# A four-layer kernel on one core: the values' pointwise products move ahead of a sample's depthwise convolutions

## The chip, the cores and the metric

The kernel runs on one core of one Trainium2 chip. Time is device microseconds (us) of that core. Before the change three runs took 4082.22, 4084.47 and 4076.9 us; the median is 4082.22 us. The profile shows one further execution, of 4084.82 us.

## The reference

Four layers act on `x` of shape (2, 128, 64, 64), each as `x = x + layer(groupnorm(x))`. The change is in layer 0:

```python
xn = biasfree_ln(x, ln1_w)
qkv = conv1x1(xn, w_qkv)                       # 128 -> 640 channels, pointwise
qkv = conv_general_dilated(qkv, w_dw, ..., feature_group_count=5 * c)   # 3x3 depthwise
q1, k1, v, q2, k2 = jnp.split(qkv, 5, axis=1)
...
q1, q2, k1, k2 = map(l2norm_tokens, (q1, q2, k1, k2))
attn1 = softmax(einsum('bhnc,bhmc->bhnm', q1, k1) * temperature)     # tokens x tokens
out1 = einsum('bhnm,bhmc->bhnc', attn1, v)
attn2 = softmax(einsum('bhnc,bhnd->bhcd', q2, k2) * temperature)     # channels x channels
out2 = einsum('bhnc,bhcd->bhnd', v, attn2)
out = conv1x1(biasfree_ln(conv1x1(out1 + out2, w_po), ln2_w), w_proj) + b_proj
```

Layer 1 is a set of small convolutions and correlations, layer 2 a quaternion product in the Fourier domain, layer 3 an attention with eight heads. The change does not touch them.

## The kernel before

Layer 0 (`_layer0`, L1449) treats the two samples one after the other. For each it normalizes the input into `xn` (channels on partitions, 4096 tokens), then runs `convolutions` (L1697), then `attention` (L1831), a long loop of TensorE, ScalarE and VectorE. `finish` (L1939) makes the output of a sample from `q1`, `v` and `w2`. For sample 0 it is not run on its own: it is the generator `before`, and sample 1's `convolutions` draws six steps of it after its first depthwise product and the rest after its second.

Inside `convolutions` each of the five groups of 128 channels is treated in two halves of 32 rows. A half takes two operations.

- `pointwise` (L1580) multiplies `xn` with the group's weights on TensorE: a halo row of 64 columns, then 512, 1024 and 512 columns. ScalarE copies each result (L1598) out of PSUM into a frame, a half with a border of zeros, which GpSimd sets by three memsets (L1582 to L1585).
- The 3x3 depthwise step is done in one of two ways. Seven halves go through TensorE (`depthwise`, L1604): 144 products with diagonal 32x32 blocks, L1613. Three halves, the first half of `k1` and both halves of `v`, go through VectorE (`taps`, L1640): a multiplication, L1648, and eight multiply-adds, L1650, on the frame.

The list `order` gives the seven TensorE halves: (1,1), (0,0), (0,1), (3,0), (4,0), (3,1), (4,1), as (group, half); groups 0 to 4 are q1, k1, v, q2 and k2. In step n of the loop TensorE does depthwise n, then the pointwise product of step n+2. A depthwise result is emptied from PSUM by ScalarE and VectorE together. For q1 and k1 `in_place` (L1626) makes sixteen copies, eight on each (L1633). For q2 and k2 `copy` (L1622, issued as L1624) makes two, one on each, into the pair `qk2`. Then ScalarE sums squares (L1638). At the end of each step VectorE does some of the taps: in sample 0, 5, 5, 5, 4, 4 and 4 of them, in sample 1, 2, 6, 6, 4, 4 and 4. One tap of `k1` is done before the first depthwise. After step 2 VectorE computes the inverse norms nq and nk (L1502, with GpSimd's power L1404) and their product `sc` (L1760), and after step 3 it scales `q1` (L1764).

PSUM has eight banks here. Six form three pairs, handed out in turn by `sp()`. Every depthwise takes two pairs, the first of them emptied by ScalarE and the second by VectorE. A pointwise product takes one pair, besides the two single banks, `acc(0)` and `acc(1)`. The other users of the pairs in this stage are the transposes of values and of the pair, and `finish` through `half()`.

In SBUF the frames for TensorE have the tag `pad` (two buffers) and the frames for VectorE the tag `vpad` (two buffers). The keys' frame takes one `vpad` buffer, so the frame of the second values' half waits for the end of the keys' taps. `qk2` has one buffer of 4096 elements, first written in step 3.

In this stage the program's own order holds on TensorE, VectorE, ScalarE and GpSimd: `_in_order` (L1328) ties each instruction to the one before it on its engine. DMAs, on SyncE's queue, are not tied in this way. The copies of layer 2's weights, L794, begin after sample 0's convolutions, whose last instruction is VectorE's product `own` (L1769).

Of the kernel before, what the change touches and what calls it, by code (L numbers as in the profile page):

```python
# [10 lines left out]
F32 = mybir.dt.float32  # L11
# [5 lines left out]
B, C, H, W = 2, 128, 64, 64  # L17
S = H * W
CH = 512
# [1429 lines left out]
def _layer0(ctx, tc, X, a, cst, worst, there, dram):  # L1449
# [13 lines left out]
    def acc(n):  # L1463
        return banks[:, 6 + n, :]
# [31 lines left out]
    v = one.tile([128, S], F32, name="v")  # L1496
# [3 lines left out]
    def inverse_norm(ss, name):  # L1500
        n = small.tile([128, 1], F32, tag=name, name=name)
        nc.vector.tensor_reduce(n, ss, AX.X, ALU.add)  # L1502
        _power(nc, small, n, n, 1e-24, 0.0, mhalf)
        return n
# [72 lines left out]
    def frame(pool, tag="pad", bufs=2):  # L1577
        return pool.tile([128, H // 2 + 2, W + 2], F32, tag=tag, name=tag, bufs=bufs)

    def pointwise(pad, grp, half):  # L1580

        nc.gpsimd.memset(pad[:, :, 0:1], 0.0)  # L1582
        nc.gpsimd.memset(pad[:, :, W + 1 : W + 2], 0.0)
        edge = 0 if half == 0 else H // 2 + 1
        nc.gpsimd.memset(pad[:, edge, :], 0.0)  # L1585
        first, to = (0, 1) if half == 0 else (H // 2 - 1, 0)
        for r0, n in ((4 * ROWS, 1), (0, ROWS), (ROWS, 2 * ROWS), (3 * ROWS, ROWS)):
            ps = sp() if n > ROWS else acc(int(r0 == 0)).rearrange("p (o c) -> p o c", o=1)
            for i in range(0, n, ROWS):
                rows = min(ROWS, n - i)  # L1590
                nc.tensor.matmul(  # L1591
                    ps[:, i // ROWS, : rows * W],
                    w_qkv[:, grp * C : (grp + 1) * C],
                    xn[:, (first + r0 + i) * W : (first + r0 + i + rows) * W],
                    start=True,
                    stop=True,
                )
            nc.scalar.copy(  # L1598
                pad[:, to + r0 : to + r0 + n, 1 : W + 1],
                ps.rearrange("p k (h w) -> p (k h) w", w=W)[:, :n, :],  # L1600
            )
            yield

    def depthwise(grp, pad):  # L1604


        ps = [sp() for _ in range(2)]
        for t in range(9):
            for c in range(4):
                for r in range(4):  # L1610
                    rows, to = slice(32 * r, 32 * r + 32), slice(32 * c, 32 * c + 32)
                    y0 = c * ROWS + t // 3
                    nc.tensor.matmul(  # L1613
                        ps[r // 2][to, r % 2, :].rearrange("p (h w) -> p h w", w=W),
                        diag[rows, grp, t, :],
                        pad[rows, y0 : y0 + ROWS, t % 3 : t % 3 + W],
                        start=(t == 0),
                        stop=(t == 8),
                    )
        return ps  # L1620

    def copy(out, in_):  # L1622
        turn[0] += 1
        (nc.scalar.copy if turn[0] % 2 else nc.vector.tensor_copy)(out, in_)  # L1624

    def in_place(ps, half, out, p):  # L1626


        for i in range(4):
            for n, engine in enumerate((nc.scalar.copy, nc.vector.tensor_copy)):  # L1630
                r, c = 2 * n + p, (i + 2 * n) % 4
                cols = slice((4 * half + c) * CH, (4 * half + c + 1) * CH)
                engine(out[32 * r : 32 * r + 32, cols], ps[n][32 * c : 32 * c + 32, p, :])  # L1633

    def squares(pool, t, at):
        junk = pool.tile([128, 2 * CH], F32, tag="junk", name="junk", bufs=1)
        n = t.free_size()
        nc.scalar.activation(junk[:, :n], t, AF.Square, accum_out=at)  # L1638

    def taps(grp, half, to, pad):  # L1640

        cols = slice(half * S // 2, (half + 1) * S // 2)
        out = to[:, cols].rearrange("p (h w) -> p h w", w=W)
        for t in range(9):
            x = pad[:, t // 3 : t // 3 + H // 2, t % 3 : t % 3 + W]
            tap = wd[:, 9 * grp + t : 9 * grp + t + 1]
            if t == 0:
                nc.vector.tensor_scalar_mul(out, x, tap)  # L1648
            else:
                nc.vector.scalar_tensor_tensor(out, x, tap, out, ALU.mult, ALU.add)  # L1650
            yield

    def squares_of(pool, out, half, at):
        for i in range(2 * half, 2 * half + 2):
            squares(pool, out[:, i * 2 * CH : (i + 1) * 2 * CH], at[:, i : i + 1])
# [41 lines left out]
    def convolutions(pool, b, before):  # L1697


        ss = small.tile([128, 2, 4], F32, tag="ss", name="ss")  # L1700
        ss2 = small.tile([128, 2, 4, 2], F32, tag="ss2", name="ss2")
        gram = None
        order = [(1, 1), (0, 0), (0, 1), (3, 0), (4, 0), (3, 1), (4, 1)]
        kpad = frame(pool, "vpad")
        run(pointwise(kpad, 1, 0))
        first = taps(1, 0, k1, kpad)
        frames = [frame(pool) for _ in range(2)]
        run(pointwise(frames[0], *order[0]))
        next(first)
        run(pointwise(frames[1], *order[1]))  # L1710
        by_vector = first

        def values_of(half):
            pad = frame(pool, "vpad")
            run(pointwise(pad, 2, half))
            return taps(2, half, v, pad)

        qk = None
        for n, (grp, half) in enumerate(order):
            ps = depthwise(grp, frames.pop(0))  # L1720
            following = iter(())
            if n + 2 < len(order):
                frames.append(frame(pool))
                following = pointwise(frames[-1], *order[n + 2])
            if grp >= 3:
                if grp == 3:
                    qk = pool.tile([128, 2, 4, CH], F32, tag="qk2", name="qk2", bufs=1)
                for p in range(2):
                    copy(qk[:, grp - 3, 2 * p : 2 * p + 2, :], ps[p])
                run(following)  # L1730
                for r in range(4):
                    squares(pool, qk[:, grp - 3, r, :], ss2[:, grp - 3, r, half : half + 1])
            else:
                out = (q1, k1)[grp]
                in_place(ps, half, out, 0)
                next(following, None)
                in_place(ps, half, out, 1)
                run(following)
                squares_of(pool, out, half, ss[:, grp, :])
            if n == 0:  # L1740
                by_vector = chain(by_vector, values_of(0))
                for _ in range(FIRST_PART):
                    next(before, None)
            elif n == 1:
                run(before)
            if n == 4:
                gram = acc(1)
                run(products(pool, qk, 0, gram))
            elif n == 5:
                run(value_tiles(0))  # L1750
            elif n == 6:
                run(value_tiles(1))
                run(products(pool, qk, 1, gram))
            if n == 2:
                squares_of(pool, k1, 0, ss[:, 1, :])
                by_vector = chain(by_vector, values_of(1))
                nq = inverse_norm(ss[:, 0, :], "nq1")
                nk = inverse_norm(ss[:, 1, :], "nk1")
                sc = small.tile([128, 1], F32, tag="sc", name="sc")
                nc.vector.scalar_tensor_tensor(sc, nq, nk, temp, ALU.mult, ALU.mult)  # L1760
            if n == 3:
                for c in range(0, NCH, 2):
                    cols = slice(c * CH, (c + 2) * CH)
                    nc.vector.tensor_scalar_mul(q1[:, cols], q1[:, cols], sc)  # L1764
            for _ in range(((5, 5, 5, 4, 4, 4, 0), (2, 6, 6, 4, 4, 4, 0))[b > 0][n]):
                next(by_vector, None)

        own = small.tile([128, 4, C], F32, tag="own", name="own", bufs=1)
        nc.vector.tensor_mul(  # L1769
            own,  # L1770
            gram.rearrange("p (r c) -> p r c", r=4),
            blocks.unsqueeze(1).to_broadcast([128, 4, C]),
        )
        return ss2, own
# [207 lines left out]
    def run(gen):  # L1982
        for _ in gen:
            pass

    def chain(*gens):
        for g in gens:
            yield from g
# [3 lines left out]
    with _in_order(tc):  # L1992
        first = normalize(0)
# [585 lines left out]
```

## Time and profile before

| What | us |
|---|---|
| median of three runs | 4082.22 |
| profiled execution, whole | 4084.82 |
| its span, first to last instruction | 4082.9 |
| start, normalization of sample 0 (0 to 33) | 33.0 |
| convolutions of sample 0 (33 to 190) | 157.0 |
| attention of sample 0 (190 to 790) | 600.0 |
| convolutions of sample 1 with the finish of sample 0 (790 to 985) | 195.0 |
| attention of sample 1 and finish (985 to 1614) | 629.0 |
| layers 1 and 2 (1614 to 2212) | 598.0 |
| layer 3 (2212 to 4083) | 1871.0 |

TensorE is busy for 95% of the span, VectorE for 78% and ScalarE for 79%. The stages are cut by hand at the rows where one kind of work gives way to another. A timeline row shows when a run of equal instructions starts, how long it is busy, engine and source line, what it writes and reads, how many there are, and in brackets how long the engine was idle before it and whose work ended that. A float32 matmul counts as two instructions, and a few matmul records can be missing.

### The profile page before, as it was taken

How to read it: one execution, taken by the hardware profiler on the slowest of the kernel's cores; microseconds unless marked ns; L12 is line 12 of the kernel's file. 1: busy time of each engine (PE TensorE's matmuls, PEld its weight loads, DVE VectorE, ACT ScalarE, POOL GpSimd, SP SyncE). 2: the span in 40 equal slices, each digit the busy share in tenths (PEclk: the TensorE clock that was granted, in tenths of full speed). 3: DMA queues.
4: the chain of work that ended last, by engine and by line, in shares of the span. 5: the costliest groups of instructions: out<-in, count | busy, mean ns of one | idle time of the engine just before them, and what ended most of it. 6: DMA issues, size and time to landing. Idle time of an engine off the chain costs nothing.

```text
span 4082.9 us, 82128 instructions
## 1 busy us (share of the span) xinstructions
PE 3876.2 (95%) x35214; PEld 1325.1 (32%) x35214; DVE 3195.3 (78%) x3572; ACT 3245.5 (79%) x3955; POOL 71.1 (2%) x145
## 2 busy tenths in 40 slices
PE   7899999989999998997898999999999999999998
PEld 4511221244111113445665232232223223222222
DVE  5699898766899998986776887777777777776666
ACT  4488888735888984334654899999999999999998
POOL 1000000010000001000000000000000000000000
PEclk9999999999999999998899999999999999999999
DMA  1199970000000000003673210121012000110000
GB/s 50 23 193 187 189 95 2 1 2 2 1 2 2 2 2 13 6 1 128 256 278 112 72 35 29 36 61 32 24 32 70 27 27 29 36 54 6 6 6 4
DMA packets 193128, 217.59 MB, mean 53 GB/s; under 512 B 30441, under 2 KB 154345, under 8 KB 188658
## 3 DMA queue, kind: packets, MB, share of 16 engines
q1 hardware_dynamic: 192754, 212.25, 20.4%
q8 instruction: 278, 4.55, 0.5%
q14 instruction: 96, 0.79, 0.1%
HBM read 178.64 MB, written 98.57 MB: 68 GB/s over the span
## 4 chain that ended last, share of the span: by engine, by line
PE 63%; DVE 8%; issue 3%; ACT 1%; SPq 0%; DMA 0%; POOL 0%; DVEq 0%; POOLq 0%; ACTq 0%
PE ps_acc L2294 25%; PE ps_s L2271 18%; PE ps L1842 5%; PE ps L1850 5%; DVE X L662 3%; PE ps_bank L710 2%; PE ps_z L1008 2%; DVE e L950 1%; DVE sums L1873 1%; PE ps_bank L1062 1%; PE ps_bank L681 1%; PE ps_acc L2152 1%; PE ps_acc L2198 1%; PE ps_pe L925 1%; ACT weights L1923 1%
## 5 line engine op out<-in xcount | busy, mean ns | idle before, releaser
L2285 ACT ACTIVATE weights<-ps_s 128x1024 f32<-128x1024 f32 x1920 | 1781.5, 1062 | 76.0 <-PE ps_s L2271 75.9
L2294 PE MATMUL ps_acc<-weights,vt 128*32 128x512 f32 x8192 | 1092.9, 605 | 0.0
L1873 DVE TENSOR_TENSOR sums<-sums,weights 128x2048 f32<-128x2048 f32 x384 | 852.1, 2284 | 0.1
L2271 PE MATMUL ps_s<-q,k 64*128 64x512 f32 x4096 | 830.3, 469 | 4.2 <-DMA k<-stack 3.0
L1923 ACT ACTIVATE weights<-ps 128x1536 f32<-128x1536 f32 x512 | 741.0, 1447 | 8.5 <-PE ps L1850 8.5
L2271 PEld LDWEIGHTS ps_s<-q,k 64*128 64x128 f32 x4096 | 348.3, 184 | 936.4 <-ACT weights L2285 809.0
L1850 PE MATMUL ps<-q,k 32*64 32x512 f32 x8192 | 574.9, 613 | 3.8 <-ACT weights L1918 3.2
L1842 PE MATMUL ps<-weights,vt 128*32 128x512 f32 x4096 | 549.0, 608 | 0.0
L2243 DVE SCALAR_TENSOR_TENSOR exp_z<-exp_z,exp_m 128x1024 f32<-128x1024 f32 x384 | 469.0, 1221 | 9.3
L1918 ACT ACTIVATE weights<-ps 128x512 f32<-128x512 f32 x512 | 306.9, 599 | 88.7 <-PE ps L1850 51.5
L2227 DVE TENSOR_SCALAR exp_i<-ps_s 128x1024 int32<-128x1024 f32 x128 | 156.7, 1225 | 216.8 <-PE ps_s L2271 216.6
L2294 PEld LDWEIGHTS ps_acc<-weights,vt 128*32 128x32 f32 x8192 | 161.9, 108 | 309.4 <-issue 308.6
L1850 PEld LDWEIGHTS ps<-q,k 32*64 32x64 f32 x8192 | 120.2, 130 | 436.2 <-ACT weights L1918 381.9
L1873 DVE TENSOR_TENSOR sums<-weights 128x2048 f32<-128x2048 f32 x64 | 146.6, 2290 | 107.0 <-ACT weights L1923 97.8
L1842 PEld LDWEIGHTS ps<-weights,vt 128*32 128x32 f32 x4096 | 85.0, 108 | 395.2 <-issue 394.2
L662 DVE SCALAR_TENSOR_TENSOR X<-g,w,X 128x2048 f32<-128x2048 f32 x84 | 197.4, 2351 | 2.6
L2247 DVE SCALAR_TENSOR_TENSOR weights<-exp_z,exp_i 128x1024 f32<-128x1024 f32 x128 | 156.8, 1225 | 15.2
L2243 DVE SCALAR_TENSOR_TENSOR exp_z<-exp_m 128x1024 f32<-128x1024 f32 x128 | 155.9, 1218 | 0.0
L1008 PE MATMUL ps_z<-w_ri,e 128*32 128x128 f32 x2048 | 137.4, 409 | 14.6 <-DVE e L950 12.4
L1613 PE MATMUL ps<-pad,diag 32*32 32x512 f32 x4032 | 141.9, 603 | 4.1 <-ACT vt L1624 3.7
L1842 PE MATMUL ps<-sums,ones 128*32 128x512 f32 x512 | 70.0, 637 | 51.0 <-DVE sums L1873 32.1
L1591 PE MATMUL ps<-xn,w_qkv 128*128 128x512 f32 (+1 forms) x200 | 91.2, 605 | 19.3 <-ACT pad L1598 14.1
(304 smaller groups left out, 2995.9 us busy)
## 6 DMA issues: line engine op xcount, KB each, us to landing
w_ri<-w_r SPq DMA_DIRECT2D x16, 2112.0 KB, 8.0
w_ri<-w_i SPq DMA_DIRECT2D x16, 2112.0 KB, 13.6
stack<-qs SPq DMA_DIRECT2D x64, 256.0 KB, 2.1
q<-stack SPq DMA_DIRECT2D x128, 128.0 KB, 2.5
k<-stack SPq DMA_DIRECT2D x128, 128.0 KB, 2.6
stack<-ks SPq DMA_DIRECT2D x32, 256.0 KB, 2.1
w_r<-in_L_conv_kr_w SPq DMA_DIRECT2D x15, 528.0 KB, 12.5
w_r<-in_L_conv_kr_x SPq DMA_DIRECT2D x15, 528.0 KB, 12.4
```

The lines of the kernel that those rows point to most:

```text
L662: nc.vector.scalar_tensor_tensor(xi, g[:, i : i + H // 2, j : j + W], w8[:, s : s + 1], xi, ALU.mult, ALU.add)
L1008: nc.tensor.matmul(out.rearrange("p (n f o) -> p n f o", n=2, f=2), e[:, s, 2 * j : 2 * j + 2, :].rearrange("p f x -> p (f x)"), w.rearran ...
L1842: nc.tensor.matmul(out[rows, :], lhs(rows), w[:, j, :], start=first, stop=stop)
L1850: nc.tensor.matmul(bank[64 * h : 64 * h + 64, :], k1[rows, kt * 128 + 64 * h : kt * 128 + 64 * h + 64], q1[rows, qb * CH : (qb + 1) * CH], ...
L1873: nc.vector.tensor_add(parts[p].rearrange("p j c -> p (j c)"), t.rearrange("p j c -> p (j c)"), w.rearrange("p j c -> p (j c)"),)
L1918: nc.scalar.activation(held[n][:, 0, :], single, AF.Exp)
L1923: nc.scalar.activation(held[n][:, 1:, :], three, AF.Exp)
L2243: nc.vector.scalar_tensor_tensor(z, x, n, m, ALU.add, ALU.mult)
L2247: nc.vector.scalar_tensor_tensor(w.rearrange("p j c -> p (j c)"), z, EXP_TERMS[-1], power, ALU.add, ALU.mult)
L2271: nc.tensor.matmul(ps[j // 2][:, j % 2, :], g.k[kt // 4][rows, j // 2, keys], g.q[qb][rows, j // 2, :], start=True, stop=True,)
L2285: nc.scalar.activation(w[0], ps[p], AF.Exp)
L2294: nc.tensor.matmul(g.ac[32 * j : 32 * j + 32, :], g.vt[:, kt, j // 2, i : i + 2, :].rearrange("p a d -> p (a d)"), w[:, i, :], start=(at = ...
```

## The change

Both pointwise products of the values now stand before the loop, after those of the keys' first half and of the first two TensorE halves. Their taps wait in a list, which becomes one chain, so that VectorE's order of taps is unchanged. The two places in the loop where they were issued before, after step 0 and after step 2, fall away. The keys' frame no longer takes a `vpad` buffer: it is laid, with the same shape, over the first 2244 elements of the buffer of `qk2`, so both values' frames have a `vpad` buffer from the start.

```diff
-        kpad = frame(pool, "vpad")
+        kpad = pool.tile([128, 8 * CH], F32, tag="qk2", name="kpad", bufs=1)
+        kpad = kpad[:, : (H // 2 + 2) * (W + 2)].rearrange("p (h w) -> p h w", w=W + 2)
         run(pointwise(kpad, 1, 0))
         first = taps(1, 0, k1, kpad)
         frames = [frame(pool) for _ in range(2)]
         run(pointwise(frames[0], *order[0]))
         next(first)
         run(pointwise(frames[1], *order[1]))
-        by_vector = first
+        by_vector = [first]
 
         def values_of(half):
             pad = frame(pool, "vpad")
             run(pointwise(pad, 2, half))
-            return taps(2, half, v, pad)
+            by_vector.append(taps(2, half, v, pad))
+
+        values_of(0)
+        values_of(1)
+        by_vector = chain(*by_vector)
...
             if n == 0:
-                by_vector = chain(by_vector, values_of(0))
                 for _ in range(FIRST_PART):
                     next(before, None)
...
                 squares_of(pool, k1, 0, ss[:, 1, :])
-                by_vector = chain(by_vector, values_of(1))
                 nq = inverse_norm(ss[:, 0, :], "nq1")
```

## The prediction

> **What bounds the kernel now.** I read the busy time by stretch first, then the timelines of TensorE and VectorE over the two convolution stages. The chain that ended last is of no help: its printed pieces begin at 974.13 us. Rows of a timeline give start and length in us; brackets give the idle time before and who ended it.
>
> ```profile
> core 0: us, PE busy (x) PEld busy (x) DVE busy (x) ACT busy (x) POOL busy (x), PEclk, DMA share, GB/s
> 33.00:190.00 157.00, 142.11 (x2294) 82.33 (x2294) 94.78 (x82) 69.05 (x127) 6.07 (x25) 0.96 0.01 2
> 790.00:985.00 195.00, 169.45 (x2486) 104.34 (x2487) 117.27 (x165) 72.30 (x132) 13.06 (x40) 0.94 0.01 2
> ```
>
> The change touches only these 352 us of 4082.9. TensorE leads in both, but neither engine is full, so the order decides. TensorE, sample 0 (L1591 is a pointwise product, L1613 a depthwise one):
>
> ```profile
> 43.28 3.92 PE L1591 MATMUL ps<-xn,w_qkv 128*128 128x64 f32 x10 [0.73 <-ACT vpad L1598]
> 47.93 3.92 PE L1591 MATMUL ps<-xn,w_qkv 128*128 128x64 f32 x10 [0.73 <-ACT pad L1598]
> 51.79 9.76 PE L1613 MATMUL ps<-pad,diag 32*32 32x512 f32 x288
> 61.48 3.92 PE L1591 MATMUL ps<-xn,w_qkv 128*128 128x64 f32 x10
> 68.58 7.09 PE L1591 MATMUL ps<-xn,w_qkv 128*128 128x64 f32 x10 [3.17 <-ACT pad L1598]
> 75.60 9.76 PE L1613 MATMUL ps<-pad,diag 32*32 32x512 f32 x288
> ...
> 90.36 10.49 PE L1613 MATMUL ps<-pad,diag 32*32 32x512 f32 x286 [0.18 <-ACT q L1633]
> ...
> 113.61 9.76 PE L1613 MATMUL ps<-pad,diag 32*32 32x512 f32 x288
> ```
>
> 68.58 is the values' first product in its old place: 65.40 to 75.60 goes to a thing that takes 4.65 us where ScalarE is free (43.28 to 47.93). VectorE, same stage:
>
> ```profile
> 61.66 5.62 DVE L1633 COPY k<-ps 32x512 f32<-32x512 f32 x8 [17.12 <-PE ps L1613]
> 67.31 11.90 DVE L1650 SCALAR_TENSOR_TENSOR k<-vpad,wd,k 128x2048 f32<-128x2048 f32 x5
> 85.47 5.62 DVE L1633 COPY q<-ps 32x512 f32<-32x512 f32 x8 [6.25 <-PE ps L1613]
> ...
> 101.85 5.62 DVE L1633 COPY q<-ps 32x512 f32<-32x512 f32 x8
> ...
> 113.59 11.90 DVE L1650 SCALAR_TENSOR_TENSOR v<-vpad,wd,v 128x2048 f32<-128x2048 f32 x5
> 125.52 1.22 DVE L1624 COPY qk<-ps 128x1024 f32<-128x1024 f32 x1
> ```
>
> Only one idle stretch, 6.25, lies between the first copies and the third, which start 1.07 late (product done at 100.78). VectorE is nearly the bound. Sample 1, from its second depthwise on:
>
> ```profile
> 878.59 14.28 DVE L1650 SCALAR_TENSOR_TENSOR k<-vpad,wd,k 128x2048 f32<-128x2048 f32 x6
> 892.90 5.62 DVE L1633 COPY q<-ps 32x512 f32<-32x512 f32 x8
> 904.49 1.28 DVE L1648 TENSOR_SCALAR v<-vpad,wd 128x2048 f32<-128x2048 f32 x1
> ```
>
> [...] the depthwise at 75.60, whose pairs of banks are free by 68.5, starts without idle time; the one at 90.36 takes its predecessor's pairs, runs two instructions at 89.14, waits and lasts 0.73 longer. [...]
>
> **The change, part by part.** Call Dn the n-th depthwise (n from 0), En its end on TensorE. Before, sample 0: E0 61.48, E1 85.28, E2 100.78, E3 123.29, E4 136.84.
>
> *Added before D0.* Two values' products at 4.65 each: E0 becomes 61.48 + 9.30 = 70.78; in sample 1, from 795.82 and 800.48, 9.32. Nothing hides it: D0 starts behind them, and VectorE's idle time of 17.12 only gets longer. ScalarE's eight copies lie in its own 9.00 idle.
>
> *Removed from the old places.* Not 9.30 but 10.20 (65.40 to 75.60) and 8.91 (104.70 to 113.61). What is late next is VectorE. The pairs of banks go round in threes, and with the two products gone from between, D1, D2 and D3 each take the two pairs of the depthwise before, one emptied by ScalarE, one by VectorE. From the row at 90.36: VectorE's copies ended at 91.09, E2 was 100.78, so a depthwise ends 9.69 after them.
>
> *Sample 0.*
> - Copies of D0: 70.96 to 76.58; E1 = 76.58 + 9.69 = 86.27 (0.99 later than before).
> - Five taps, 11.90: to 88.51, past E1. Copies of D1 88.53 to 94.13 (before 91.09); E2 = 103.82 (+3.04).
> - Taps 7.13 + 1.28 + 2.35, end to end 10.73: copies of D2 at 104.88, to 110.5 (+3.03). E3 = 110.5 + 9.69 = 120.2, 3.1 earlier.
> - The norms wait for ScalarE's squares, which follow E2 and these copies: VectorE's taps start at 116.63 instead of 113.59. The copy of D3 stands behind them: 128.56 to 129.78. D4 takes D3's pairs: E4 = 129.8 + 9.69 = 139.5 instead of 136.84, **2.65 us later**. The 3.1 of E3 are lost here.
> - From the pair's first token tiles on, TensorE (TensorE row at 140.59, no idle before it) hands the 2.65 on unchanged; VectorE's copy of D4 ends at 141.8, before 143.2, when it is wanted.
>
> In sum: VectorE gains its 6.25 idle and pays 9.30, and 3.05 less what D4 makes up is left.
>
> *Sample 1.* The finish of sample 0 stands between D0 and D1. Its first statistics on VectorE (828.56, idle 8.73 before it, released by TensorE L1963) came 14.54 after E0 (814.02), since the values' product stood ahead. Now TensorE reaches its first product 3.9 after E0, VectorE is done with its copies at 5.83, and 3.9 + 1.99 (826.57 to 828.56) gives 5.86. Gain 8.68, price 9.32: everything to E2 is 0.6 later. At D3 TensorE gains 6.9 (VectorE's copies end at 898.5, D3 started at 904.53), but the taps at 904.49 and the copy of D3 at 917.74 are VectorE's own chain, 0.62 later, to 919.58. E4 = 919.6 + 9.69 = 929.3, as before (929.29). Net 0.
>
> *Edits that cost nothing.* The memsets of the values' frames (three of 0.16 each half) go ahead of GpSimd's power at 12.38, by which time it had been idle for 9.78; in sample 1 they wait for the totals' matmuls (to 792.3), some 12 us before they are needed. The keys' frame in the pair's buffer: its taps end before 105, the pair is first written at 120, and no wait comes of it; the first exponential now lands over the pair and waits for TensorE's last transposes (187.3 instead of 186.56), while TensorE comes to the next scores only at 190.25: 2 us of cover. SP's copies of the weights, released by the end of sample 0's convolutions (L1769), start 2.65 later and run beside 600 us of attention. Not shown by the trace: taps reading the new address. The same operation on two other frames takes 2.35 each; I take no change, at most 1 us either way for 9 taps a sample.
>
> **Sum.** 2.65 + 0.0. The profiled execution took 4084.82 (span 4082.9); it would take 4087.5. The median of the runs, 4082.22, lies 2.60 below that execution: **4084.9**, 0.07% slower, inside the 0.2% (8.2 us) that a measurement of this kernel tells from no change.
>
> **The rivals.**
> - *Faster: TensorE is the bound, VectorE only seems late.* Then the copies of D3 come right after E3 and E4 follows by 13.55, as before (123.29 to 136.84). Sample 0 without lateness: E2 = 86.27 + 15.50 = 101.77, E3 = 101.77 + 15.50 = 117.3, E4 = 130.8: 6.0 earlier. Sample 1: E3 908.8, E4 922.4: 6.9 earlier. Together 12.9: 4069.3. For it: the idle times of 3.17 before each values' product. Against it: five taps of 11.90 stand ahead of that copy in VectorE's order. Chance 0.05.
> - *Slower: the finish in sample 1 doesn't move up.* If its first statistics wait for something else than the values' product, ScalarE's squares, say (which end 9.3 after E0), the 9.32 are not given back: VectorE's copy of D3 ends at 928.3, E4 at 938.0, 8.7 later, total 4093.6. It decides from 5.5 us of delay there. Against it: ScalarE's first part in the finish comes 3.99 after the statistics (832.55), at 9.8, when it is free. Chance 0.08.
> - *The moved products hide, VectorE starts its taps earlier.* If the keys' taps ran in VectorE's 17.12 of idle time, D2's and D3's copies would come early and part of the 6 us of the first rival's sample 0 would be had: some 4078. But the order has only one tap before D0's copies: chance 0.02.
>
> **How the numbers follow.** The forecast has 0.83, with 4081 to 4089 as its own range (1.5 for the working; the runs of before spread from 4076.9 to 4084.47). Faster by over 0.2% takes the first rival's 0.05; slower the second's 0.08 and 0.02 for a wait I don't see; within 0.2% are the forecast and the third rival, 0.85. The range 4079 to 4091 leaves out the first rival and most of the second, and holds the price of the address.
>
> **What would show it.** D0 at 61.1 instead of 51.79; D1 starting some 5.8 after E0 instead of 14.1; VectorE without its 6.25; the copy of D3 at 128.6 with TensorE waiting for it in D4; sample 1's first statistics 5.9 after E0. The forecast falls if VectorE's copy of D3 isn't what D4 waits for, or if the first statistics don't move up.

## The result, and the profile after

| | before | after |
|---|---|---|
| median, us (13 runs each) | 4081.45 | 4092.49 |
| lowest to highest, us | 4075.65 to 4091.03 | 4085.86 to 4099.56 |
| profiled execution, us | 4084.82 | 4092.49 |
| its span, us | 4082.9 | 4090.7 |

The ratio is 1.0023, with a 95% interval of 1.0014 to 1.0032 (the two medians alone give 1.0027): the changed kernel is 0.23% slower. The interval lies on both sides of the 0.2% that counts as a difference here. The forecast was 4084.9 us with a range to 4091, so the time lies 1.5 us above the range.

Spans also differ by what the change doesn't touch: in the profiled executions of all the kernels below, the time after sample 1's convolutions runs from 3094 to 3107 us. So I compare the two stages themselves, each from the start of the keys' first tap (L1648) to the start of VectorE's product `own`, the stage's last instruction.

| us | before | after | change | forecast |
|---|---|---|---|---|
| convolutions of sample 0 | 147.09 | 154.74 | +7.65 | +2.65 |
| convolutions of sample 1 | 188.59 | 189.36 | +0.77 | 0 |

These 8.42 us, less 1.31 by which sample 0's stage began earlier and with 0.69 elsewhere, are the 7.8 between the two spans. So the question is where 5.00 us in sample 0 and 0.77 in sample 1 come from. First TensorE's timeline after the change, sample 0 (rows as in the prediction; times are 1.31 early against its figures):

```profile
59.80 9.76 PE L1613 MATMUL ps<-pad,diag 32*32 32x512 f32 x288
...
74.55 10.48 PE L1613 MATMUL ps<-pad,diag 32*32 32x512 f32 x286 [0.18 <-ACT k L1633]
...
90.04 1.09 PE L1613 MATMUL ps<-pad,diag 32*32 32x512 f32 x4 [0.17 <-ACT q L1633]
92.91 12.32 PE L1613 MATMUL ps<-pad,diag 32*32 32x512 f32 x282 [1.79 <-DVE q L1633]
105.17 3.92 PE L1591 MATMUL ps<-xn,w_qkv 128*128 128x64 f32 x10
...
124.44 1.05 PE L1613 MATMUL ps<-pad,diag 32*32 32x512 f32 x4
131.19 12.09 PE L1613 MATMUL ps<-pad,diag 32*32 32x512 f32 x284 [5.71 <-DVE qk L1624]
143.21 3.92 PE L1591 MATMUL ps<-xn,w_qkv 128*128 128x64 f32 x10
```

From here on products are counted as the rows count them, two for each float32 product (288 for the 144 of a depthwise). D0 and D1 are as forecast. D2 waits 1.79 for VectorE's copies, to 92.91, and then its remaining 282 products take 12.32 instead of 9.7 (9.70 in the run with the waits filled, below). D4 waits 5.71 for VectorE's copy of D3, and its 284 take 12.09. VectorE, same stretch:

```profile
69.66 5.62 DVE L1633 COPY k<-ps 32x512 f32<-32x512 f32 x8 [26.42 <-PE ps L1613]
...
87.24 5.62 DVE L1633 COPY q<-ps 32x512 f32<-32x512 f32 x8
...
105.28 5.62 DVE L1633 COPY q<-ps 32x512 f32<-32x512 f32 x8 [1.68 <-PE ps L1613]
...
117.99 11.89 DVE L1650 SCALAR_TENSOR_TENSOR v<-vpad,wd,v 128x2048 f32<-128x2048 f32 x5
129.91 1.23 DVE L1624 COPY qk<-ps 128x1024 f32<-128x1024 f32 x1
```

The copies at 87.24 have lost the 6.25 of idle time, as forecast. Those at 105.28 wait 1.68 for TensorE, which was not forecast: D2 is late. Why the same products take longer is seen in the granted clock. Windows of the same execution, each 3.41 us long, as is the shortest stretch of half clock in this stage (173.92 to 177.33), and laid on the times at which half clock begins (columns: stretch and length, then busy time and instructions by engine, then the TensorE clock, 1.00 being full):

```profile
core 0: us, PE busy (x) PEld busy (x) DVE busy (x) ACT busy (x) POOL busy (x), PEclk, DMA share, GB/s
88.59:92.00 3.41, 2.36 (x7) 0.31 (x6) 3.33 (x6) 3.35 (x6) 0.00 (x0) 1.00 0.00 0
92.00:95.41 3.41, 2.50 (x48) 1.05 (x64) 3.33 (x4) 2.31 (x5) 0.00 (x0) 0.50 0.02 5
95.41:98.82 3.41, 3.41 (x72) 1.69 (x47) 3.38 (x2) 0.00 (x0) 0.00 (x0) 0.50 0.00 0
...
126.13:129.54 3.41, 0.00 (x0) 0.00 (x0) 3.37 (x2) 0.43 (x2) 0.00 (x0) 1.00 0.00 0
129.54:132.95 3.41, 1.75 (x33) 0.51 (x34) 3.38 (x5) 1.45 (x4) 0.00 (x0) 0.50 0.00 0
```

In the first window TensorE does seven instructions (six of them D2's first products, which the profile counts as 2.1 us of work; D0 does 288 in 9.76), and in the two windows after it the clock is 0.50. The same happens round D4: a window with nothing in it, then 0.50 to 136.36. If products go at half speed there, those from 92.91 to 98.82 and from 131.19 to 136.36 lose half of 5.91 and of 5.17, an estimate of 2.95 and 2.6; the rows lost 2.6 and 2.4. In sample 1 it is D3 and D4, with the clock at 0.50 from 904.37 to 911.20 and from 924.85 to 931.68:

```profile
905.70 12.24 PE L1613 MATMUL ps<-pad,diag 32*32 32x512 f32 x282 [1.78 <-DVE q L1633]
...
926.16 12.25 PE L1613 MATMUL ps<-pad,diag 32*32 32x512 f32 x284 [3.39 <-DVE qk L1624]
```

The kernel before has such intervals too. Its values' product at 68.58, which the prediction shows with 7.09 us where its equals take 3.92, lies in one, from 68.17 to 75.00. Windows of before:

```profile
64.76:68.17 3.41, 0.64 (x2) 0.00 (x0) 3.34 (x5) 3.35 (x6) 0.00 (x0) 1.00 0.00 0
68.17:71.58 3.41, 3.00 (x5) 1.60 (x6) 3.37 (x2) 3.11 (x7) 0.00 (x0) 0.50 0.01 2
```

So before, TensorE's waits stood ahead of ten pointwise products, and the half clock fell on these; after, the waits stand inside a depthwise, and it falls on 280 dense products.

### The profile page after: what moved, and what is told of

It is laid out like the page before. It is cut to its first block, busy times and chain, and to the rows that moved or that the text cites. A ratio compares the mean times of both kernels' runs of the same rounds, so it can differ in the third digit from the quotient of the medians.

```text
span 4090.7 us, 82123 instructions
## 1 busy us (share of the span) xinstructions
PE 3878.9 (95%) x35214; PEld 1323.2 (32%) x35214; DVE 3195.5 (78%) x3572; ACT 3246.8 (79%) x3955; POOL 70.8 (2%) x145
## 4 chain that ended last, share of the span: by engine, by line
PE 65%; DVE 5%; issue 3%; ACT 2%; DMA 0%; SPq 0%; POOL 0%; POOLq 0%; DVEq 0%; ACTq 0%
PE ps_acc L2297 24%; PE ps_s L2274 18%; PE ps L1845 5%; PE ps L1853 5%; PE ps_bank L710 2%; PE ps_z L1008 2%; DVE e L950 1%; PE ps_t L640 1%; DVE sums L1876 1%; PE ps_bank L590 1%; PE ps_bank L681 1%; PE ps_bank L1062 1%; PE ps_acc L2155 1%; PE ps_acc L2201 1%; PE ps_pe L925 1%
## 5 line engine op out<-in xcount | busy, mean ns | idle before, releaser
L1613 PE MATMUL ps<-pad,diag 32*32 32x512 f32 x4032 | 162.4, 652 | 19.4 <-DVE qk L1624 9.1
L1613 PEld LDWEIGHTS ps<-pad,diag 32*32 32x32 f32 x4032 | 91.3, 107 | 85.3 <-issue 28.3
```

The lines of the kernel that those rows point to most:

```text
L1613: nc.tensor.matmul(ps[r // 2][to, r % 2, :].rearrange("p (h w) -> p h w", w=W), diag[rows, grp, t, :], pad[rows, y0 : y0 + ROWS, t % 3 : t ...
```

## The experiments

Theory 1: VectorE's copies hold TensorE up inside D2, D3 and D4, and after these waits the granted clock falls to half. Theory 2: the keys' frame in the pair's buffer costs time. Theory 3: TensorE is the bound, and each product moved ahead of D0 is simply paid. The medians of before beside these runs were 4080.58, 4081.48 and 4081.78 us. The two last columns are stage lengths of the profiled execution, less those of before (147.09 and 188.59):

| run | median, us | ratio to before, 95% interval | sample 0 | sample 1 |
|---|---|---|---|---|
| after | 4092.49 | 1.0023 [1.0014, 1.0032] | +7.7 | +0.8 |
| keys' frame alone | 4079.82 | 0.9997 [0.9987, 1.0006] | +0.1 | +0.9 |
| after, waits filled | 4087.59 | 1.0013 [1.0004, 1.0021] | +4.2 | +0.1 |
| first half early | 4075.23 | 0.9987 [0.9980, 0.9994] | +1.5 | -5.8 |
| second half early | 4093.28 | 1.0027 [1.0017, 1.0036] | +4.2 | +4.7 |
| after, keys' taps early | 4062.15 | 0.9959 [0.9946, 0.9973] | -4.8 | -13.8 |
| before, keys' taps early | 4070.31 | 0.9975 [0.9968, 0.9982] | -1.7 | -9.2 |
| first half and keys' taps early | 4064.68 | 0.9962 [0.9948, 0.9976] | -3.7 | -13.1 |
| before, copy of D3 late | 4090.39 | 1.0022 [1.0013, 1.0031] | +7.7 | 0.0 |
| after, two taps behind the copy of D3 | 4081.52 | 0.9998 [0.9990, 1.0006] | -0.4 | -6.3 |

### The keys' frame alone

```diff
-        kpad = frame(pool, "vpad")
+        kpad = pool.tile([128, 8 * CH], F32, tag="qk2", name="kpad", bufs=1)
+        kpad = kpad[:, : (H // 2 + 2) * (W + 2)].rearrange("p (h w) -> p h w", w=W + 2)
```

> The kernel before with one part of the change: the keys' frame in the pair's buffer, the values' products in their old places. Theory 1 (VectorE's copies hold TensorE up, and TensorE's granted clock falls to half after those waits, now inside depthwise products): nothing, ratio 0.999 to 1.001, depthwise products of 9.7 us but where the kernel before has other lengths. Theory 2 (the buffer costs, by slower taps or a wait of the pair): most of the change's 9 us, ratio 1.002, taps over 2.35 us each or a wait at the pair's first copy.

Measured: 0.9997, with an interval that holds 1. In the changed kernel five of the keys' taps from the new address take 11.90 us, as before. Theory 2 falls.

### The waits filled with repeated products

In the changed kernel TensorE repeats some first products of D2 and D4 in sample 0, of D3 and D4 in sample 1, while it waits; each repeat is a sum of its own (`start` and `stop` set), and the true products start theirs again at the same place.

```diff
+        for _ in range(again):
+            for c in range(4):
+                for r in rr:
...
+                    nc.tensor.matmul(
+                        ps[r // 2][to, r % 2, :].rearrange("p (h w) -> p h w", w=W),
+                        diag[rows, grp, 0, :],
...
-            ps = depthwise(grp, frames.pop(0))
+            ps = depthwise(grp, frames.pop(0), *AGAIN[b].get(n, ()))
```

> The changed kernel, with the first products of a depthwise issued again (same inputs, same place, overwritten) to fill TensorE's waits: 3 rounds of 4 ahead of D2 and 6 of 8 ahead of D4 in sample 0, 6 of 4 ahead of D3 and 4 of 8 ahead of D4 in sample 1. Theory 1: with TensorE busy the clock stays at 1.0, D2 and D4 of sample 0 and D3 and D4 of sample 1 last 9.7 to 10.5 instead of 12.1 to 12.3; 5 us less in sample 0 and 2.5 to 5 less in sample 1 than the changed kernel: ratio to before 1.000 to 1.001. If instead the clock has no part and only the banks are waited for: no gain, up to 2 us more where the filling overshoots: ratio 1.002 to 1.003.

Measured: 1.0013. TensorE's rows in sample 0:

```profile
92.26 9.70 PE L1625 MATMUL ps<-pad,diag 32*32 32x512 f32 x282 [0.47 <-DVE q L1645]
...
127.32 10.33 PE L1625 MATMUL ps<-pad,diag 32*32 32x512 f32 x288
```

D2 and D4 are back at about their old length, though TensorE has more to do, and no half-clock interval lies in either. From the first tap on, D4 ends 96.3 us later instead of 101.3: 5.0 less, the 2.6 and 2.4 of the rows after. At the stage's end 3.4 of these 5.0 are left, since the half clock there falls on the pair's products (145.75 to 149.25), which it did not in the profiled execution of after. In sample 1, D3 was still slow (an interval from 900 to 907), and little was won. The forecast had D4 end 96.2 us after the first tap (139.5 less 43.26): with VectorE's copy of D3 as late as forecast (to 86.6 us after the first tap, forecast 86.5) and the clock whole, it does. This shows the clock as the missing term there. The ratio lies between the two expectations and its interval overlaps that of after, so it decides nothing; the rows do.

In sample 1 the repeats ahead of D3 use, like those ahead of D2, one of the four strips of rows, four of the sixteen blocks that a tap of a depthwise has. The profile has TensorE busy through the whole of the window ahead of the slow stretch, and the next one is at half all the same:

```profile
896.74:900.15 3.41, 3.41 (x38) 0.91 (x30) 3.34 (x5) 0.91 (x2) 0.00 (x0) 1.00 0.00 0
900.15:903.57 3.42, 2.80 (x35) 0.63 (x34) 1.44 (x3) 1.83 (x3) 0.00 (x0) 0.50 0.01 2
```

So repeats that the profile calls busy need not keep the clock whole: D0 does about 100 instructions in such a time (288 in 9.76), and here there are 38.

### One half of the values at a time

Against the changed kernel, first with the second half's product back behind step 2, then with the first half's back behind step 0; the order of the taps stays:

```diff
-            by_vector.append(taps(2, half, v, pad))
+            return taps(2, half, v, pad)
...
-        values_of(0)
-        values_of(1)
-        by_vector = chain(*by_vector)
+        by_vector = chain(first, values_of(0))
...
                 squares_of(pool, k1, 0, ss[:, 1, :])
+                by_vector = chain(by_vector, values_of(1))
```

```diff
-        values_of(0)
-        values_of(1)
-        by_vector = chain(*by_vector)
+        by_vector, last_half = first, values_of(1)
...
             if n == 0:
+                by_vector = chain(by_vector, values_of(0), last_half)
```

> The changed kernel, but only the first half of the values is ahead of the depthwise products; the second stays after step 2. Theory 1: sample 0, E0 4.65 later, copies of D0 end at 71.9, E1 81.6, copies of D1 end at 89.5, E2 99.2, 1.6 earlier than before, and from there as before, but for a clock drop of 2.5 in D2; sample 1, the finish moves up by 8.7 for 4.65, 4 us earlier; together 3 to 5 us faster than before, ratio 0.9985 to 0.9995. Theory 3 (each product moved ahead is simply paid): 2 times 4.65 slower, ratio 1.0023.

> The changed kernel, but only the second half of the values is ahead; the first stays after step 0. Theory 1: sample 0, everything to E2 4.65 later, D3 earlier by 1.5, but VectorE's copy of D3 4.65 later, so that E4 is 4.3 later, and 2.4 for the clock in D4; sample 1 the same way 4.0 and 2.5; together 13 slower, ratio 1.003. Theory 3: 9.3 slower, ratio 1.0023.

Measured: the first half alone is faster than before (0.9987), the second alone slower (1.0027; 8.9 us in the two stages, where 13 were expected). Sample 1 shows both parts of the forecast's sum there. With the first half early, VectorE's copies of D0 begin 22.97 after the first tap instead of 18.34 (the price of one product, 4.63), but those of D1 follow 32.64 later instead of 41.34: the finish moves up by 8.70, for which the forecast had 8.68. With the second half early, the price is the same, and D1's copies follow after 41.32, as before: nothing is given back, and the stage is 4.7 longer. So it is the first half's product that made the finish wait, and one price buys the whole gain. In sample 0 each half costs, 1.5 and 4.2, partly by half clock (D2's 282 products took 11.24 with the first half early; D3's and D4's took 11.30 and 11.32 with the second). Theory 3 falls: two equal products have opposite prices.

### The keys' taps early

In both kernels, eight of the keys' nine taps go ahead of D0's copies, into VectorE's idle time (26.42 in the row at 69.66 above), and fewer stand between the depthwises:

```diff
-        next(first)
+        for _ in range(8):
+            next(first)
...
-            for _ in range(((5, 5, 5, 4, 4, 4, 0), (2, 6, 6, 4, 4, 4, 0))[b > 0][n]):
+            for _ in range(((4, 4, 2, 3, 3, 3, 0), (1, 4, 2, 4, 4, 4, 0))[b > 0][n]):
```

> The changed kernel, but VectorE does eight of the keys' nine taps (instead of one) before the copies of D0, in the 26 us in which it is idle there, and fewer taps between the depthwises (4, 4, 2, 3, 3, 3 in sample 0; 1, 4, 2, 4, 4, 4 in sample 1). Theory 1 (VectorE's late copies, and the half clock that follows TensorE's wait for them, eat the gain of the move): sample 0, by the rows of after: copies of D1 at 85.0 instead of 87.24, E2 100.3 (105.17), E3 115.8 (120.6), the copy of D3 ends at 119.1, before D4 wants the pair, E4 129.5 instead of 143.2, 6.0 earlier than before the change; sample 1 some 12 earlier than before the change. About 18 us faster than before, ratio 0.9956; 0.998 if the clock falls elsewhere instead. Theory 3 (each product moved ahead is simply paid, TensorE is the bound): no change against after, ratio 1.002.

> The same earlier taps in the kernel before, with the values' products in their old places. Theory 1: sample 0 hardly moves, since there TensorE stands behind ScalarE's copies of the values and not behind VectorE (147 us as before); sample 1 up to 5.2 us shorter; ratio 0.9987. The move of the products is then worth about -13 us with the taps early (e5 less this), where it cost +9 without. Theory 3: the move costs +9 us here too, so this kernel is at least 9 us faster than e5.

> Only the first values' product early, with the earlier taps. Theory 1: in sample 0 D2 no longer waits for VectorE's copies (1.79 us there without the earlier taps, and 1.5 of half clock after it): 3 to 4 us less than with the first product early alone; sample 1 2 to 5 less. Ratio 0.997, slower than e5, since the second product still stands behind ScalarE's copies. Theory 3: no change against the first product early alone, ratio 0.9987.

Measured: 0.9959 with both halves early, 0.9975 with the values in their old places, 0.9962 with the first half early. TensorE and one copy of VectorE, sample 0, both halves early:

```profile
87.33 10.42 PE L1613 MATMUL ps<-pad,diag 32*32 32x512 f32 x286 [0.17 <-ACT q L1633]
...
116.96 9.77 PE L1613 MATMUL ps<-pad,diag 32*32 32x512 f32 x288
```

```profile
115.25 1.23 DVE L1624 COPY qk<-ps 128x1024 f32<-128x1024 f32 x1
```

D2 waits 0.17 instead of 1.79. D4 starts at 116.96, just behind the copy of D3 (to 116.48), and waits for nothing. No half clock lies between 40 and 134 us of this execution, and sample 1 has two intervals of it instead of before's six of one or two windows each. Theory 1 gave 0.9956. The kernel before gains more from the earlier taps than I expected, 9.2 in sample 1 instead of 5.2: I had left out that its copy of D3 no longer stands behind five taps, and that its D3 (11.29 before) then runs at the full clock (9.76). So the move of the values, which costs 8.4 us in the two stages with the taps late, is worth 7.7 us with the taps early (142.3 and 174.8 against 145.4 and 179.4), not the 13 expected; in ratios 0.9959 against 0.9975, some 6.5 us, and their intervals overlap a little. Both halves and the first half alone can't be told apart.

### The wait alone, in the kernel before

```diff
+                if n == 3 and b == 0:
+                    for _ in range(11):
+                        nc.vector.tensor_copy(v[:, : 2 * CH], v[:, : 2 * CH])
                 for p in range(2):
                     copy(qk[:, grp - 3, 2 * p : 2 * p + 2, :], ps[p])
```

> The kernel before, with one thing more: in sample 0 VectorE copies 128x1024 of the values onto themselves eleven times just ahead of its copy of D3, about 7.5 us at 0.68 each. D4 (at 127.15 before, 9.76 long, clock whole) must then wait some 6 us in its first products, as in the changed kernel, with nothing of the change. Theory 1: the clock is halved for one or two intervals after the wait, D4's remaining 284 products take 12.1 instead of 9.7, and the stage grows by 7.1 + 2.4 = 9.5 us, ratio 1.0023. Without a price of the clock (the long D2 and D4 have to do with the frames or the order): 9.7, 7.1 us, ratio 1.0017.

Measured: 1.0022, with an interval that holds both expected ratios; the rows decide. VectorE and TensorE:

```profile
118.55 7.97 DVE L1730 COPY v<-v 128x1024 f32<-128x1024 f32 x11
```

```profile
127.84 11.33 PE L1613 MATMUL ps<-pad,diag 32*32 32x512 f32 x284 [6.61 <-DVE qk L1624]
```

The eleven copies took 0.72 each, not the 0.68 of the estimate. A wait of 6.61 in D4 and nothing else of the change makes the same products take 11.33: 1.6 of half clock (an interval from 124.44 to 131.27, of which 3.43 lie on D4; half of that is 1.7). The expected 12.1 came out smaller, because less of the interval was left when D4 went on. The stage is 7.7 longer and not 9.5: in this execution the first values' product ran at the full clock (3.92 at 64.77, against before's 7.09 at 68.58), 3.2 less ahead of D4, and other intervals took part of that back behind it.

### The wait of D4 alone taken away

```diff
-            for _ in range(((5, 5, 5, 4, 4, 4, 0), (2, 6, 6, 4, 4, 4, 0))[b > 0][n]):
+            for _ in range(((5, 5, 3, 4, 5, 5, 0), (2, 6, 4, 4, 5, 5, 0))[b > 0][n]):
```

> The changed kernel, with two of the five or six taps that stand ahead of VectorE's copy of D3 put behind it (5, 5, 3, 4, 5, 5 taps after the depthwises of sample 0; 2, 6, 4, 4, 5, 5 in sample 1; the keys' taps stay late). It takes away TensorE's wait in D4 alone; the waits in D2 of sample 0 and D3 of sample 1 stay. Theory 1: sample 0, from the rows of after: taps at 117.99, three of them 7.1 us, copy of D3 to 126.4 instead of 131.1; D4's wait falls from 5.71 to under 1, and its products from 12.09 to 9.7: E4 at 136.1 to 136.5 instead of 143.21, 7 us. Sample 1: copy of D3 4.7 earlier, D4's wait of 3.39 gone, 12.25 becomes 9.8, E4 6 to 7 earlier. D2 (12.3) and D3 (12.2) stay long. About 13 us less than after, ratio 0.999. If VectorE's copy of D3 isn't what holds D4 (the rival with TensorE as the bound), E4 and the total don't move: 1.002. If the half clock hits D4 whatever its wait: 9 us less, 1.000.

Measured: 0.9998, 15.1 us less than after in the two stages and 10 by the ratios. TensorE, sample 0:

```profile
93.15 9.71 PE L1613 MATMUL ps<-pad,diag 32*32 32x512 f32 x282 [1.79 <-DVE q L1633]
...
123.03 10.72 PE L1613 MATMUL ps<-pad,diag 32*32 32x512 f32 x288
```

VectorE's copy of D3 now ends at 123.97, 0.94 after D4's first product, and D4 takes 10.72: 0.96 over the 9.76 of an unhindered one, with no half clock in it. So the copy of D3 was what held D4. (The ratio alone would also fit the expectation that the half clock hits D4 whatever its wait; the row rules that out.) And D2, with the very wait of 1.79 that cost 2.6 in the execution of after, takes 9.71. I had expected 12.3. Its window, from the grid on which this execution's clock changes:

```profile
91.76:95.17 3.41, 2.02 (x66) 1.01 (x68) 3.36 (x3) 2.43 (x4) 0.00 (x0) 1.00 0.02 5
```

The wait, to 93.15, is followed by 2.02 us of work within the same window, and the next window's clock stays full. The first half early had again the same wait of 1.79, at another place on the grid:

```profile
83.60:87.02 3.42, 1.63 (x51) 0.76 (x65) 3.36 (x4) 2.43 (x5) 0.00 (x0) 1.00 0.03 5
87.02:90.43 3.41, 3.41 (x71) 1.89 (x50) 3.34 (x3) 0.99 (x2) 0.00 (x0) 0.50 0.00 0
```

With 1.63 busy, the next window is at half, once: D2 took 11.24. So one wait of 1.79 cost 2.6, 1.5 and 0 in three executions. In all three D2 had in fact been held for 4.09 us, from its first product to its seventh (88.82 to 92.91 in after): the rows count the six products in between as 2.13 us of work.

## Why the prediction was right in its mechanism and missed its range

The forecast named the right waits and the right sign, and made the loss too small: +2.65 us in the two stages, where 8.42 were measured. Point by point (forecast less the 1.31 of the earlier start in sample 0, plus the 6.50 by which sample 1's stage began later):

| step | forecast, us | measured, us |
|---|---|---|
| sample 0: copies of D0 begin | 69.65 | 69.66 |
| E1 | 84.96 | 84.97 |
| copies of D1 begin | 87.22 | 87.24 |
| E2 | 102.51 | 105.17 |
| E3 | 118.89 | 120.59 |
| VectorE's taps after the norms | 115.32 | 117.99 |
| end of the copy of D3 | 128.47 | 131.14 |
| E4 | 138.19 | 143.21 |
| sample 1: first statistics after E0 | 5.86 | 5.82 |
| D2 later by | 0.6 | 0.64 |
| end of the copy of D3 | 926.08 | 926.11 |
| E4 | 935.8 | 938.3 |

- **Added before D0.** Right: 4.63 a half.
- **Removed from the old places; what is late next is VectorE.** Right: the waits named are there, D4's on the copy of D3. The run with two taps put behind that copy shows that it decides; the faster rival, with TensorE as the bound, falls.
- **The step that failed: "a depthwise ends 9.69 after them".** The 9.69 came from one row, at 90.36, whose wait was 0.18. It holds for D1 and D3 of sample 0 (E3 is 9.69 after copies that end at 110.90). In D2 and D4, whose waits the forecast itself named, the same stretch took 12.3 and 12.1: 2.66 late at E2, which comes down the chain as 2.67 at the copy of D3, and 2.35 more in D4. 2.67 + 2.35 = 5.02, and at the stage's end the miss is 5.00. That nothing changes behind E4 is luck: before, half clock lay on the pair's products there (146.68 to 150.09) and D6's 284 products took 9.73; after, the pair ran at the full clock and D6 took 11.32. In sample 1 the same step gave 9.69 for D4 and measured 12.25. Of these 2.6 only 0.77 is left at the end, and that too is luck: the kernel before loses 1.65 and 1.63 to half clock on the pair's products (938.57 to 941.98 and 976.12 to 979.53), after loses 1.5 on D6 instead.
- **The finish of sample 0 moves up.** Right to 0.04 us, so the slower rival, which has it not move, is not what happened, though its total of 4093.6 is near the measured time.
- **Edits that cost nothing.** Right: 0.9997 for the keys' frame alone.

- **The moved products hide, VectorE starts its taps earlier.** This rival was given 4078 us at a chance of 0.02, since the order has one tap there. With the order of the taps changed to that, the kernel takes 4062.15.

The mechanism was right and one term was put at nothing, without a reason: the lower speed at which TensorE can go on after a wait (282 products in 12.32 instead of 9.70 us, with the clock at 0.50). It was to be read from the profile: the row at 68.58 has 7.09 us for ten products that take 3.92 elsewhere, and the prediction showed it and counted the difference as time "removed". It was the price of the wait of 3.17 ahead of it, and the waits were not removed but moved.

In the two stages of before and after, half clock lasts one or two windows of 3.413 us at a time (3.41 or 6.83), and on a fixed grid: in after it begins at 92.00, 129.54 and 173.92, 11 and 13 times 3.413 apart. Each time TensorE was busy for at most 2.36 us of the window ahead of it. That does not make it a rule: the window of before from 870.30 to 873.72, with 1.71 busy, was followed by the full clock, and the wholly busy one at 896.74 in the run with the waits filled by half.

What stays open: the price is not fixed; at three places on the grid the wait of 1.79 cost 2.6, 1.5 and 0 us. The kernel before pays such a price as well, and at other places from one execution to the next (the first values' product took 7.09 us in before, and 3.92 in the run with the copy of D3 late, whose edit comes behind it). The 7.65 of sample 0 is one execution's account; the 9.4 us of the ratio (0.0023 of 4081.45) are near its total of 8.4, but how often D2 pays was not measured.

## What to carry to other kernels

Equal groups of instructions with unequal durations, here 3.92, 5.81 and 7.09 for ten products, can be the mark of a lower granted clock (here 0.50 from 109.13 to 112.54 for the second, from 68.17 to 75.00 for the third): look at the clock by windows and for the wait ahead of them, and price a new wait of TensorE by its length plus what half clock may cost after it (here 0 to 2.6 us, in one or two windows of 3.41). When work leaves an engine's gaps, look which engine was covered by it; here VectorE was, and the gain of the move could be had once VectorE's own idle time at the stage's start was filled (4062.15 us against 4081.48). Of two equal parts of a change, try each alone: one bought the whole gain here, the other only paid.

## What the hardware showed that was not expected

- No limit in TensorE's busy time tells which window is followed by half clock. Of D2's windows above, the one with 1.63 was and the one with 2.02 was not. But in the run with the first half early, D6's window with 1.59 (162.11 to 165.52) was followed by the full clock, and two windows of D6 in the kernel before with the keys' taps early, nearly alike in what they hold, went one each way (each with the window after it):

```profile
158.59:162.00 3.41, 1.57 (x51) 0.74 (x65) 3.38 (x3) 1.96 (x5) 0.00 (x0) 1.00 0.00 0
162.00:165.41 3.41, 3.41 (x70) 1.88 (x49) 3.37 (x2) 0.00 (x0) 0.00 (x0) 0.50 0.02 5
943.65:947.06 3.41, 1.56 (x51) 0.82 (x65) 3.38 (x3) 1.82 (x5) 0.00 (x0) 1.00 0.02 5
947.06:950.47 3.41, 3.41 (x128) 2.19 (x101) 3.38 (x2) 0.00 (x0) 0.00 (x0) 1.00 0.00 0
```

- A window counted as busy for 2.36 us (88.59, above) was followed by half too: 2.13 us of it were six single products (two in 1.04 at 88.82, four in 1.09 at 90.04), where a full depthwise does 288 in 9.76. So busy time in the profile is not what the clock goes by. What it goes by, no run here shows.
- Half clock lasted for two windows where the first of them was only partly busy (2.50 and 1.75 of 3.41 in D2 and D4 of after), and for one where that one was busy throughout (D2 with the first half early).
- The same wait of 1.85 us in D6 of sample 1 (behind ScalarE's copies of the values' tiles) was followed by 11.22 us for 284 products in after and by 9.72 in before.
